# Two attention blocks over eight images: a new order for VectorE's work between attentions, and key-tile sums by transfers in every attention

## The chip, the cores and the metric

The kernel runs on one core of a Trainium2 chip. The metric is the device time of one execution in microseconds (us), the median of several runs. The profile is of one such execution.

## The reference

The input is eight images of 512 channels by 1024 positions, in float32. Two blocks follow each other, with the same computation and different weights:

```python
xn = group_norm(x, 8 groups) * gamma + beta
q, k, v = Wq @ xn + bq, Wk @ xn + bk, Wv @ xn + bv        # 512 x 1024 each
attn = softmax(q^T k / sqrt(64))                          # 8 heads of 64, 1024 x 1024 each
x = x + Wp @ (v attn^T) + bp
```

So there are 16 jobs, an image and a layer each. The kernel goes through them by pairs of images: layer 0 of both, then layer 1 of both.

## The kernel before

**Stages.** A job has a stage of projections and an attention. From job 3 on one stage of projections, called phase n here, makes v of job n, the output projection of job n-1, and k and q of job n, in this order. Every 512x512x1024 product is done with a two-level Strassen-Winograd scheme: seven outer products, each of which is a *chain* of seven inner ones. Phase n has 28 chains: 0 to 6 make v, 7 to 13 the output, 14 to 20 k, 21 to 27 q. Two neighbouring chains are interleaved product by product on TensorE. A product takes some 0.43 us of TensorE.

**A chain** (`chain`, and `deep_phases` with `begin`, `end`, `product` and `put`). Its products come in the order 1, 5, 6, 2, 7, 3, 4 and accumulate in four PSUM banks z, y, u, w. ScalarE copies z to y after product 1, w to an SBUF tile `s5` after product 5 (L780) and z to u after product 6 (L470), and evicts two of the four blocks (L760, L769, L771). In an output, k or q chain VectorE evicts the other two and adds `s5` to them (L776, L778): the block of z after product 7, and the block of u after product 3. Product 4 accumulates in z again, so it waits for VectorE's eviction after product 7; three other products of the interleaved chains stand between the two. In a v chain ScalarE evicts all four, and VectorE adds `s5` once at the end (`add_five`, L801). `s5` comes from a pool of three buffers.

**VectorE's other work in a phase.** The seven chains' results are added to each other in tiles of 128x1024: for v by `plus` (L805, queued in `values`), for the output, k and q by `add` and `more` (L792, L832, queued in `outer`). The output's chains need sums of the attention's result: `plan_sums` lists them in `planned` with a time before which they may not be done, a time by which they are to be done, and the chain before which they must be done (L413 to L419, and L562 to L567 in the tile `os`). Some of the output's parts are added to x by an accumulating transfer on GpSimd's queue instead (L830).

**What sets the order.** The engines' orders are written by hand: the Python code runs along TensorE's products and keeps a `clock` that `advance` moves. `pump` puts VectorE's next work into its queue as long as VectorE is free, by its planned costs, before `clock + AHEAD` (0.8 us). `spend` books those costs: 1.14 us a 128x1024 addition, 0.62 us an `add_five`. VectorE counts as busy for `TAIL` = 9.0 us from the phase's start. `pump` is called at every product of a v chain, and after products 7 and 3 of the other chains. `p_tile` calls for work ahead of its time where no tile is free.

**Attention** (class `Attention`, `run`). It has 64 steps, in 8 groups of 8 key tiles; a group is a pair of heads and half of the queries. In step i TensorE makes the scores of key tile i (L1029) and the values of key tile i-2 (L1080), and ScalarE makes `e`, the exponential (L1034). The softmax's denominators need the sum of the eight `e` of a group. Either VectorE does seven additions (L1048, L1050), or, where `by_transfer` holds, two pairs of the first four `e` are added by an accumulating transfer on GpSimd's queue (`add_pair`, L1057, 512 KB), VectorE adds the other four, and adds the two sums of pairs five steps after each transfer was issued (`LANDING` = 5, L1060). `by_transfer` holds from attention 4 on, but not for the last group of an attention. Then `reduce` (L1115) and the steps after it turn the sum into a factor, which comes back over DRAM on SP's queue to a tile `rb`, and `normalise` multiplies (L1172).

**Buffers.** `e`, the weights of the chains (`w`), the chains' results (`p`) and the weights of `deep_values` share one pool of 12 tiles of 128x1024. `deep_values` prepares the v weights of a layer during attentions 2 and 3: seven times a load, four VectorE additions (L159 to L165) and a store to DRAM. SP's queue issues all loads of weights, the stores of the output and the loads of the next images, in the order of the code.

Of the kernel before, what the change touches and what calls it, by code (L numbers as in the profile page):

```python
# [47 lines left out]
PARTS = 6  # L48
LANDING = 5
BLOCK = {1: (0, 0), 2: (0, 1), 4: (1, 1)}  # L50
AHEAD, TAIL = 0.8, 9.0
PLACE = {2: (0, 0), 6: (0, 1), 5: (1, 1), 7: (1, 0)}
DEEP_V = 3
OUTER_V = (1, 6, 7, 2, 3, 5, 4)
# [24 lines left out]
def fast_path(  # L79
# [522 lines left out]
    def deep_phases(n, extra, outs=None, early=()):  # L602
# [28 lines left out]
        def spend(us):  # L631
            free_at[0] = max(free_at[0], clock[0]) + us

        def next_work(c, forced=False):
            now = clock[0] - began[0] if began else 0.0
            if planned and planned[0][1] <= now and not forced:
                _, _, _, us, fn = planned.popleft()
            elif values:
                us, fn = values.popleft()
            elif planned and planned[0][0] <= now and not forced:  # L640
                _, _, _, us, fn = planned.popleft()
            elif outer:
                fn = outer.popleft()
                us = 0.0 if fn in free else 1.14
            elif extra and extra[0][0] <= c - base:
                us, fn = 0.65, extra.popleft()[1]
            else:
                return False
            fn()
            spend(us)  # L650
            return True

        def pump(c):
            while free_at[0] < clock[0] + AHEAD and next_work(c):
                pass

        def plan_sums():
# [124 lines left out]
        def end(c):  # L782
            which, o = chains[c]
            m = job(which)
            used((m, which, o))

            def p(k):
                return tiles[which, k]

            def add(to_, a, b, frees):  # L790
                def go():
                    nc.vector.tensor_add(to_, a, b)  # L792
                    let_go((which, frees))

                outer.append(go)

            if which == V:
                def add_five():
                    to_ = p(o)[:, 2:4, :].rearrange("p t (o c) -> p t o c", o=2)
                    five = fives[V, o].rearrange("p (t c) -> p t c", t=2).unsqueeze(2)  # L800
                    nc.vector.tensor_add(to_, to_, five.to_broadcast([P, 2, 2, P]))  # L801

                def plus(to_, a):
                    def go():
                        nc.vector.tensor_add(p(to_), p(to_), p(a))  # L805
                        let_go((V, a))

                    values.append((1.14, go))

                values.append((0.62, add_five))  # L810
                for to_, a in {
                    6: ((6, 1),), 7: ((7, 6),), 2: ((2, 1),), 3: ((6, 3),), 5: ((6, 5), (5, 7)),
                    4: ((7, 4),),
                }.get(o, ()):
                    plus(to_, a)
                return

            if which == O:
                b, layer = jobs[m]
                xt = xs[b]  # L820

                def more(oh, sh, part, moved=False):


                    cols = slice(sh * HALF, (sh + 1) * HALF)
                    to_ = xt[:, 2 * oh : 2 * oh + 2, cols]

# [13 lines left out]

                    waiting[oh, sh] += 1
                    if not moved:
                        outer.append(go)
                    elif waiting[oh, sh] == 1:
                        go()
                    else:
                        outer.append(go)
                        free.append(go)

                if o == 1:
                    more(0, 0, 1, m > 0)
                elif o == 2:
                    more(0, 0, 2, True)
                elif o == 6:
                    add(p(6), p(6), p(1), 1)
                    more(0, 1, 6)
                elif o == 5:
                    more(0, 1, 5)
                    more(1, 1, 5, m in (0, 2))  # L860
                elif o == 7:
                    add(p(7), p(7), p(6), 6)
                    more(1, 0, 7)
                    more(1, 1, 7)
# [11 lines left out]
        waiting, free = dict.fromkeys(parts, 0), []  # L876
        soon, outer = deque(early), deque()

        def thunk(c, j):
            def go():  # L880
                if with_v and not began:
                    began.append(clock[0])
                    free_at[0] = clock[0] + TAIL
                if j == 0:
                    live[c] = begin(c)
                order = LAST_ORDER if c + 1 == len(chains) else ORDER
                live[c](order[j])
                if with_v:
                    if chains[c][0] == V:
                        pump(c)  # L890
                    elif order[j] in (7, 3):
# [17 lines left out]
                advance(0.446 if chains[c][0] == V else 0.432)  # L909

            return go

        for which, o in chains[:2]:
            prepare((job(which), which, o))
# [10 lines left out]
        return [thunk(c, j) for c, j in at], plan_sums  # L925

    def last_weights(n):
        w = acts.tile([P, NW, 2, CH], F32, tag="deep", name="w_last")
# [78 lines left out]
    class Attention:  # L1007
        def __init__(self, n):
# [7 lines left out]
            self.spread = n > DEEP_V  # L1016
            self.summed, self.due = {}, {}

        def scores(self, i, tag="sc"):
# [18 lines left out]

        def add(self, i):
            g, kc = self.steps[i]  # L1040
            if self.by_transfer(g):
                if kc < NT // 2:
                    return
                kc -= NT // 2
            acc, e = self.acc, self.es[i]
            if kc == 1:
                acc[g] = apool.tile([P, 2, HALF], F32, tag="acc", name=f"acc_{self.n}_{g}")
                nc.vector.tensor_add(acc[g], self.es[i - 1], e)  # L1048
            elif kc > 1:
                nc.vector.tensor_add(acc[g], acc[g], e)  # L1050

        def by_transfer(self, g):
            return self.spread and g + 1 < len(self.groups)

        def add_pair(self, i):
            g, kc = self.steps[i]
# [1 line left out]

            def add():
                nc.vector.tensor_add(self.acc[g], self.acc[g], self.summed.pop(i))  # L1060
                if kc == NT // 2 - 1:
                    self.reduce(g)

            self.due[i + LEAD + LANDING] = add
# [1 line left out]
        def values(self, i):  # L1066
# [4 lines left out]
            if kc == 0:  # L1071
                po[g] = two_banks("po", f"po_{n}_{g}")
            e = es.pop(i)
            if self.by_transfer(g) and kc < NT // 2:
                self.summed[i] = e
            for h in range(2):
                r = slice(h * HD, (h + 1) * HD)
# [7 lines left out]
        def finish(self, g):  # L1085
# [3 lines left out]


            self.take(g)
            if not self.by_transfer(g):
                self.reduce(g)

        def take(self, g, middle=None):
# [82 lines left out]
        def run(self, chores, between=None, middle=None):  # L1178
# [8 lines left out]
            for i in range(3, len(steps) + LEAD):  # L1187
# [3 lines left out]
                    between()  # L1191
                self.values(i - LEAD)
                g, kc = steps[i - LEAD]
                if self.by_transfer(g) and kc in (1, 3):
                    self.add_pair(i - LEAD)
                if i in self.due:
                    self.due.pop(i)()
# [286 lines left out]
    for n in range(-1, len(jobs)):  # L1484
        last = n + 1 == len(jobs)
        outs = None
        if n >= 0:
# [369 lines left out]
```

## Time and profile before

| | us |
|---|---|
| median of 3 runs (lowest, highest) | 3270.77 (3269.48, 3271.94) |
| the profiled execution | 3270.5 |
| its span, from first to last instruction | 3268.7 |
| VectorE, ScalarE busy | 2728.4, 2077.0 |
| mean granted TensorE clock | 0.992 |

A row of stretches gives for each stretch: its borders, its length, and for each engine the busy time with the number of instructions; then the mean granted clock of TensorE as a share of full speed, the busy share of the 16 DMA engines and what they moved. A row of waits has the waiting engine and line, who ended the wait, the total in us, how often, and the longest. A row of the timeline has start, duration, engine, line, operation, tiles and shapes; in brackets is the engine's idle time before it and who ended that.

Attention n ends where phase n+1 begins; the first products of the phase are mixed into the attention's last steps.

### The profile page before, as it was taken

To read this page: it belongs to the slowest core of one execution; us is meant where nothing else is said; L and a number is where in the kernel's file an instruction comes from. 1 tells how busy PE (TensorE), PEld (TensorE's weight loads), DVE (VectorE), ACT (ScalarE), POOL (GpSimd) and SP (SyncE) were. 2 spreads that over 40 slices of the span, in tenths; PEclk is the share of its full clock that TensorE was granted. 3 is DMA by queue.
4 is the path that set the end of the run, shared out by engine and by line. 5 is a ranking of instruction groups with operands and counts; after the bars stand their busy time and mean duration, and the time that the engine had idled before them with its cause. 6 is when DMAs were issued, how large, how long until landed. Compare 5 with 4: busy or idle time off the path is not lost. (4 is left out here: it accounts for less than half of the span.)

```text
span 3268.7 us, 61316 instructions
## 1 busy us (share of the span) xinstructions
PE 3197.8 (98%) x24009; PEld 1883.6 (58%) x24009; DVE 2728.4 (83%) x4008; ACT 2077.0 (64%) x3583; POOL 233.2 (7%) x262
## 2 busy tenths in 40 slices
PE   9999999899999999999999999999999999999999
PEld 7365483563846638366483654837547375573744
DVE  8897999989879787897978879788797887978867
ACT  4746656565666666666666666666666666666664
POOL 0000000000010010100001000010000100001000
PEclk9999999999999999999999999999999999999999
DMA  7243352443645454455554545445556453444643
GB/s 269 67 130 97 98 174 83 155 146 107 196 89 143 107 137 132 80 154 145 143 173 91 147 98 140 116 92 163 139 134 176 91 174 83 133 118 93 192 106 80
DMA packets 180746, 424.11 MB, mean 130 GB/s; under 512 B 37224, under 2 KB 55264, under 8 KB 180192
## 3 DMA queue, kind: packets, MB, share of 16 engines
q1 hardware_dynamic: 139664, 300.04, 27.7%
q0 software_dynamic: 40784, 120.08, 20.3%
q8 instruction: 190, 3.11, 0.4%
q14 instruction: 108, 0.88, 0.1%
HBM read 246.69 MB, written 52.10 MB: 91 GB/s over the span
## 5 line engine op out<-in xcount | busy, mean ns | idle before, releaser
L1034 ACT ACTIVATE e<-sc 128x1024 f32<-128x1024 f32 x1024 | 1043.7, 1024 | 582.8 <-PE sc L1029 518.6
L1029 PE MATMUL sc<-q,k 64*64 64x512 f32 x8192 | 1062.2, 591 | 15.2 <-ACT e L1034 14.9
L1080 PE MATMUL po<-e,v 64*64 64x512 f32 x8192 | 1062.8, 591 | 0.0
L1029 PEld LDWEIGHTS sc<-q,k 64*64 64x64 f32 x8192 | 311.3, 133 | 582.1 <-issue 515.5
L1080 PEld LDWEIGHTS po<-e,v 64*64 64x64 f32 x8192 | 312.7, 133 | 562.7 <-issue 548.5
L1050 DVE TENSOR_TENSOR acc<-acc,e 128x1024 f32<-128x1024 f32 x432 | 525.5, 1216 | 50.5 <-ACT e L1034 35.0
L1048 DVE TENSOR_TENSOR acc<-e,e 128x1024 f32<-128x1024 f32 x128 | 156.3, 1221 | 123.4 <-ACT e L1034 123.2
L753 PE MATMUL zd<-deep,w 128*128 128x256 f32 x860 | 241.3, 380 | 2.7 <-DVE p L776 1.9
L1057 POOL DMA_DIRECT2D e<-e x168 | 144.5, 860 | 1174.1 <-ACT e L1034 1007.6
L753 PE MATMUL vd<-deep,w 128*128 128x256 f32 x804 | 224.5, 380 | 3.7 <-ACT yd L466 1.5
L1060 DVE TENSOR_TENSOR acc<-acc,e 128x1024 f32<-128x1024 f32 x168 | 204.1, 1215 | 1.3
L753 PEld LDWEIGHTS zd<-deep,w 128*128 128x128 f32 x860 | 162.8, 190 | 27.4 <-DVE p L776 3.1
L830 POOL DMA_DIRECT2D x<-p x61 | 73.4, 1203 | 1386.6 <-ACT p L771 602.5
L753 PEld LDWEIGHTS vd<-deep,w 128*128 128x128 f32 x804 | 152.2, 190 | 26.9 <-ACT yd L466 1.9
L1115 DVE TRANSPOSE_TENSOR_REDUCE r<-acc 128x32 f32<-128x1024 f32 x128 | 159.0, 1243 | 3.3
L753 PE MATMUL zd<-os,w 128*128 128x256 f32 x352 | 100.1, 385 | 33.1 <-DVE p L776 31.5
L780 ACT COPY s<-zd 128x256 f32<-128x256 f32 x209 | 77.9, 373 | 84.9 <-PE zd L753 65.0
L780 ACT COPY s<-vd 128x256 f32<-128x256 f32 x195 | 72.7, 373 | 81.9 <-PE vd L753 58.4
L470 ACT COPY ud<-vd 128x256 f32<-128x256 f32 x209 | 74.6, 357 | 78.4 <-PE vd L753 73.9
L753 PE MATMUL vd<-os,w 128*128 128x256 f32 x368 | 114.9, 397 | 4.0 <-DVE p L778 3.9
L470 ACT COPY ud<-zd 128x256 f32<-128x256 f32 x195 | 70.0, 359 | 70.8 <-PE zd L753 69.6
L748 PE MATMUL vd<-w,deep 128*128 128x128 f32 x780 | 113.1, 278 | 0.0
(308 smaller groups left out, 4725.3 us busy)
## 6 DMA issues: line engine op xcount, KB each, us to landing
w<-deep SPq DMA_DIRECT2D x378, 448.0 KB
e<-e POOLq DMA_DIRECT2D x168, 512.0 KB, 4.6
x<-p POOLq DMA_DIRECT2D x61, 512.0 KB, 5.6
rb<-rd SPq DMA_DIRECT2D x96, 256.0 KB
deep<-w SPq DMA_DIRECT2D x42, 448.0 KB
x<-x_dram SPq DMA_DIRECT2D x28, 512.0 KB
out_dram<-x SPq DMA_DIRECT2D x28, 512.0 KB
w<-keep SPq DMA_DIRECT2D x32, 256.0 KB
```

Of the source, the lines that this page charges most:

```text
L470: nc.scalar.copy(u, z)
L748: nc.tensor.matmul(ps[:, tokens], moving[i][:, tokens], lhs[:, FACTOR[i], :], start=(start and ti == 0), stop=True, skip_group_check=True,)
L753: nc.tensor.matmul(ps, lhs[:, FACTOR[i], :], moving[i], start=start, stop=True, skip_group_check=True,)
L780: return chain(product, lambda ps: nc.scalar.copy(s5, ps), put, z, y, u, w)
L1029: nc.tensor.matmul(sc[h * HD : (h + 1) * HD, j, :], k[r, hp, k0 : k0 + HD], q[r, hp, sh * HALF : (sh + 1) * HALF], start=True, stop=True,)
L1034: nc.scalar.activation(e, sc, AF.Exp, scale=SCALE)
L1048: nc.vector.tensor_add(acc[g], self.es[i - 1], e)
L1050: nc.vector.tensor_add(acc[g], acc[g], e)
L1057: nc.gpsimd.dma_start(self.summed[i], self.summed.pop(i - 1), accum_op=ALU.add)
L1060: nc.vector.tensor_add(self.acc[g], self.acc[g], self.summed.pop(i))
L1080: nc.tensor.matmul(po[g][j * HD : (j + 1) * HD, h, :], v[r, kc, d0 : d0 + HD], e[r, j, :], start=(kc == 0), stop=(kc == NT - 1),)
L1115: nc.vector.tensor_reduce(self.r[:, 0, m, :], self.acc.pop(g).rearrange("p j (b e) -> p (j b) e", e=RP), AX.X, ALU.add, apply_transpose=True,)
```

## The change

In the phases from job 3 on:

- VectorE counts as busy for 12.0 us from the start, a 128x1024 addition is booked with 1.22 us, an `add_five` with 0.72 us.
- `pump` is called at every product of every chain, with a limit: the time up to which VectorE has to be free for its next eviction after a product 7, plus `SLACK` = 1.3 us. Work of `values`, `outer` and `extra` that doesn't fit before the limit is not placed; the planned sums are not held back by it.
- The `add_five` of chains 0 and 1 are placed at once.

In the attentions: two pairs of every group but the last are summed by transfers in every attention, also in 0 to 3. In the last attention four additions for the last projection are placed three steps later each.

```diff
-AHEAD, TAIL = 0.8, 9.0
+AHEAD, TAIL, SLACK = 0.8, 12.0, 1.3
-        def next_work(c, forced=False):
+        def next_work(c, forced=False, limit=None):
             now = clock[0] - began[0] if began else 0.0
+            room = 9.9 if limit is None else limit - max(free_at[0], clock[0])
...
             elif values:
+                if values[0][0] > room:
+                    return False
                 us, fn = values.popleft()
...
             elif outer:
+                if room < 1.22 and outer[0] not in free:
+                    return False
                 fn = outer.popleft()
-                us = 0.0 if fn in free else 1.14
-            elif extra and extra[0][0] <= c - base:
+                us = 0.0 if fn in free else 1.22
+            elif extra and extra[0][0] <= c - base and room > 0.65:
...
-        def pump(c):
-            while free_at[0] < clock[0] + AHEAD and next_work(c):
+        def pump(c, limit):
+            while free_at[0] < clock[0] + AHEAD and next_work(c, limit=limit):
...
-                    values.append((1.14, go))
-
-                values.append((0.62, add_five))
+                    values.append((1.22, go))
+
+                if c < 2:
+                    add_five()
+                    spend(0.72)
+                else:
+                    values.append((0.72, add_five))
...
-                    if chains[c][0] == V:
-                        pump(c)
-                    elif order[j] in (7, 3):
+                    if chains[c][0] != V and order[j] in (7, 3):
                         spend(0.38)
-                        pump(c)
+                    pump(c, limits[i] and clock[0] + limits[i])
...
+        limits, limit = [], None
+        for c, j in reversed(at):
+            limits.append(limit)
+            if chains[c][0] != V and (LAST_ORDER if c + 1 == len(chains) else ORDER)[j] == 7:
+                limit = takes(c) + SLACK
+            if limit is not None:
+                limit += takes(c)
+        limits.reverse()
...
-        def by_transfer(self, g):
-            return self.spread and g + 1 < len(self.groups)
+        def pairs(self, g):
+            return 0 if g + 1 == len(self.groups) else 2
...
-                    put(46 + 3 * i, fn)
+                    put(49 + 3 * i, fn)
```

More of the change, by code (lines that the diff above doesn't have):

```diff
@@ L806, in go @@
                         let_go((V, a))
-                    values.append((1.14, go))
-                values.append((0.62, add_five))
-                for to_, a in {
+                    values.append((1.22, go))
[4 more added lines that the diff above has]
+                    values.append((0.72, add_five))
+                for step in {
                     6: ((6, 1),), 7: ((7, 6),), 2: ((2, 1),), 3: ((6, 3),), 5: ((6, 5), (5, 7)),
@@ L814, in end @@
                 }.get(o, ()):
-                    plus(to_, a)
+                    plus(*step)
                 return
@@ L877, in deep_phases, with thunk @@
         soon, outer = deque(early), deque()
-        def thunk(c, j):
+        def thunk(i, c, j):
             def go():
@@ L908, in go, with takes @@
                         assert not values and not planned
-                advance(0.446 if chains[c][0] == V else 0.432)
+                advance(takes(c))
             return go
+        def takes(c):
+            return 0.446 if chains[c][0] == V else 0.432
         for which, o in chains[:2]:
@@ L924, in deep_phases @@
             ]
-        return [thunk(c, j) for c, j in at], plan_sums
+        limits, limit = [], None
[6 more added lines that the diff above has]
+        limits.reverse()
+        return [thunk(i, c, j) for i, (c, j) in enumerate(at)], plan_sums
     def last_weights(n):
@@ L1015, in __init__ @@
             self.es, self.acc, self.po = {}, {}, {}
-            self.spread = n > DEEP_V
             self.summed, self.due = {}, {}
@@ L1040, in add @@
             g, kc = self.steps[i]
[L1041 to L1044, printed above, removed]
+            first = 2 * self.pairs(g)
+            if kc < first:
+                return
+            kc -= first
             acc, e = self.acc, self.es[i]
@@ L1060, in add @@
                 nc.vector.tensor_add(self.acc[g], self.acc[g], self.summed.pop(i))
-                if kc == NT // 2 - 1:
+                if kc == 2 * self.pairs(g) - 1:
                     self.reduce(g)
@@ L1073, in values @@
             e = es.pop(i)
-            if self.by_transfer(g) and kc < NT // 2:
+            if kc < 2 * self.pairs(g):
                 self.summed[i] = e
@@ L1091, in finish @@
             self.take(g)
-            if not self.by_transfer(g):
+            if not self.pairs(g):
                 self.reduce(g)
@@ L1193, in run @@
                 g, kc = steps[i - LEAD]
-                if self.by_transfer(g) and kc in (1, 3):
+                if kc % 2 == 1 and kc < 2 * self.pairs(g):
                     self.add_pair(i - LEAD)
```

## The prediction

> **What bounds the kernel now.** I read the page's shares first, then the waits, then stretches stage by stage, then the timeline where a wait stood. TensorE is busy almost all of the span:
>
> ```profile
> PE 3197.8 (98%) x24009; PEld 1883.6 (58%) x24009; DVE 2728.4 (83%) x4008; ACT 2077.0 (64%) x3583; POOL 233.2 (7%) x262
> ```
>
> Its products are the same, in the same order, in both kernels, and so is ScalarE's work. So the change can win only what TensorE loses now: some 71 us idle, and time at a lower clock. The waits name two places:
>
> ```profile
> PE zd L753 <- DVE p L776: 34.0, 16, 3.8
> PE sc L1029 <- ACT e L1034: 14.9, 6, 4.7
> ACT e L1034 <- DVE acc L1050: 18.7, 14, 5.1
> ACT e L1034 <- DMA deep<-w_values: 6.8, 3, 5.1
> ```
>
> The first is a product 4 of a chain that waits for VectorE's eviction; the others are scores that wait for ScalarE, and ScalarE for a tile that VectorE or a store still holds. The stretches tell which stages pay. They are attentions 2, 3 and 4, then phases 4, 6 and 3:
>
> ```profile
> 489.80:608.80 119.00, 111.41 (x1018) 38.80 (x1017) 112.75 (x153) 73.01 (x76) 1.43 (x1) 0.99 0.34 111
> 701.10:822.70 121.60, 114.25 (x1018) 39.42 (x1017) 115.66 (x157) 73.06 (x76) 1.42 (x1) 0.96 0.28 86
> 910.70:1019.90 109.20, 109.20 (x1018) 38.79 (x1017) 93.22 (x114) 73.32 (x76) 12.60 (x15) 1.00 0.50 109
> 824.80:910.70 85.90, 85.51 (x490) 76.69 (x486) 67.43 (x116) 58.69 (x154) 4.80 (x4) 1.00 0.60 176
> 1223.30:1313.40 90.10, 87.37 (x490) 78.01 (x490) 69.96 (x119) 58.22 (x154) 4.80 (x4) 0.98 0.45 128
> 610.90:701.20 90.30, 85.80 (x490) 76.58 (x488) 73.66 (x146) 58.70 (x154) 6.00 (x5) 1.00 0.64 198
> ```
>
> The same work takes 109.2 us in attention 4, where TensorE never stops, and 9.8 and 12.4 us more in attentions 2 and 3, where VectorE is busy 95% (112.75 of 119.00). Attentions 0 and 1 take 110.1 us with TensorE busy throughout. Phase 4 takes 85.9 us, phase 6 4.2 us more. The eleven phases 5 to 15, by the same stretches, last 991.7 us together, against 11 x 85.9 = 944.9: 46.8 us more. In the timeline of phase 6 this has one place:
>
> ```profile
> 1247.67 0.68 DVE L801 TENSOR_TENSOR v<-v,s 128x512 f32<-128x512 f32 x1
> 1248.45 2.48 DVE L805 TENSOR_TENSOR v<-v 128x1024 f32<-128x1024 f32 x2
> 1250.86 0.42 DVE L776 TENSOR_TENSOR p<-zd,s 128x256 f32<-128x256 f32 x1
> ```
>
> ```profile
> 1251.33 0.70 PE L753 MATMUL zd<-os,w 128*128 128x256 f32 x2 [2.48 <-DVE p L776]
> ```
>
> VectorE, without a pause since the attention's tail, does three items of v before the first output chain's eviction (1250.86), and product 4 waits 2.48 us.
>
> **The price of such a stall** is more than its length: the four us after it are at a lower clock.
>
> ```profile
> 1251.30:1255.40 4.10, 4.07 (x13) 3.36 (x14) 2.68 (x5) 1.57 (x4) 1.20 (x1) 0.67 0.09 16
> ```
>
> Clock 0.67 for 4.1 us loses 1.35 us by the clock; against phase 4, product by product, it is 1.67 us. The Trainium skill ("TensorE: Matmul & The Clock Gate", Part 1 on the clock gate) has the clock drop only after an idle window of about 3.4 us. By that a 2.48 us stall costs only itself, and eleven phases could win 11 x 2.5 = 27 us. The stretches give 46.8; I take them.
>
> **The order of VectorE, phases 5 to 15.** Nothing is added or removed; I walked the new order with the distances from start to start that this timeline shows (128x1024: 1.14 us, 1.2 where two follow on one tile; `add_five` 0.60, or 0.79 if its sum follows; `os` 0.34 to 0.45; evictions 0.34 and 0.40), beside the product times of stall-free phase 4. Up to the first `add_five` (1232.67) the order is the old one. The three items above (3.19 us) move behind the eviction, so VectorE is free for it at 1250.86 - 3.19 = 1247.67. Product 7 ends at about 1247.5 and product 4 is wanted at 1248.85: the eviction ends at 1248.1, and the stall goes.
>
> What is late next: the `add_five` of chain 3 moves from 1240.87 to 1242.1, that of chain 4 from 1244.27 to 1245.3. They hold `s5`, so ScalarE's copies of `s5` of chains 6 and 7, now at 1241.87 and 1245.04, come at 1242.9 and 1246.0. Behind each stand an eviction and the copy of z to u (0.37 us each) that product 7 waits for: ready at 1244.0 and 1247.15, wanted at 1243.8 and 1246.85. That is 0.25 and 0.35 us. The `add_five` of chain 5 now stands behind chain 8's evictions, so chains 7, 8 and 9 share one `s5` buffer, and ScalarE's copy waits for the chain before; there 0.2 to 0.35 us are left. Chain 11's eviction has two sums of v before it, 0.13 us late; the later ones with two 128x1024 before them (chains 14, 15, 19, 26) end with 0.05 us to spare. Sum: 0.7 us a phase. Bounds: 0, if the stalls absorb each other, and 2.
>
> Queues that this passes: the additions to x come some 7 us earlier beside the products, so the accumulating transfers and the output's stores too. With them the four loads of the next image, in the phases that have them, now stand in SP's queue ahead of four loads of q weights. In phase 4 the last transfer would land at about 881 instead of 887.7; a store takes 4.6 us (887.7 to 892.3), so the loads go out at 885.5. In phase 7 these 2 MB and two weights (448 KB each) were in 10.4 us after the first issue (1496.1 to 1506.5, where the DMA share falls); 2 MB and one weight scale to 9 us, so they land at 894.5; chain 24 wants them at 897.2. So it costs 0, and up to 2 us in each of six phases if transfer and store are both slow.
>
> Phases 5 to 15: 46.8 - 11 x 0.7 = 39.1 us won. Phase 4 has no stall now, since attention 3 before it left VectorE free earlier; with that attention changed its tail is like the others': 0.7 lost. Phase 3 has seven preparations of weights (L159 to L165, 1 us each) that the plan doesn't book: the walk gives stalls of 2.6, 1.2, 0.7, 0.6 and 0.7 us, 5.8 together, where it now has 3.8. 2.0 lost.
>
> **Attentions 0 to 3.** In seven groups of each, seven additions become five: 14 x 1.216 = 17.0 us less VectorE work. In attentions 0 and 1 that is worth nothing, TensorE hides it. In 2 and 3 VectorE comes to 95.8 and 98.7 us of 109.2, beside 93.2 in attention 4, which has no stall. From the timelines, the running sum there begins up to 12 us behind the `e` it adds (group 6), in attention 4 at most 4. The four preparations of v weights in the last groups (0.96 us each) are what attention 4 lacks, so I expect a lag of 5 to 6 us. A weak point stays: the exponential of step 57 takes the tile of a prepared weight whose store is issued only at step 54 or so; with a lag of 3 us and a store of 3 us ScalarE waits 1 to 2 us. I take 1 us of TensorE in each: (9.8 - 1) + (12.4 - 1) = 20.2 won; bounds 8 and 22.
>
> 56 more transfers go through GpSimd's queue (0.86 us each, engine idle); what could be late is their landing, for VectorE waits for it in order, five steps (8.55 us) after the issue:
>
> ```profile
> e<-e POOLq DMA_DIRECT2D x168, 512.0 KB, 4.6
> DMA to landing us min/median/max: 4.5/4.6/7.2
> ```
>
> The Trainium skill ("DMA: Bandwidth & Descriptors", SWDGE vs HWDGE vs iDMA) speaks against it: an engine alternates between queues of GpSimd and of SP, and attentions 0 to 2 begin with 1 to 2 MB of weights. Twice 4.6 is 9.2, 0.65 too late. But those loads are over 10 us into the attention (DMA share 0.73 up to 93 us, 0.01 after it), and the first sum is wanted 14 us in. Free VectorE time covers the rest.
>
> SP's small loads of factors fall behind one store or weight load each in attentions 0 to 3, and the last attention's four additions come three steps later: VectorE's freed time and TensorE's last products cover both; 0.5 us without that.
>
> **Sum.** The profiled execution took 3270.5 us, 1.8 around its span, 0.3 under the median. 39.1 - 0.7 - 2.0 + 20.2 = 56.6 less is 3213.9, in terms of the median 3214.
>
> **Rivals.** *The stall only moves* (0.08). If VectorE runs 1 us later than walked, the late `s5` copies stop TensorE at chains 6 to 9 by 1 us each: phases win nothing, 3270.5 - 20.2 + 2.7 = 3253. For it: margins of 0.2 us. Against: the walk gives 2.5 us for the present stall, and VectorE works 70 of 90 us.
> *Attentions 2 and 3 stay bound* (0.12): by tiles, not by VectorE. For it: the 5.1 us wait for a store. Against: that store was late because VectorE was. 8 instead of 20.2: 3226.
> *Slower* (0.04): the transfers of attentions 0 to 3 land late. VectorE there averages 108.1 - 17.0 = 91.1 us busy; to lose the phases' 36.4 us each must last 115.2 + 9.1 = 124.3, so 33 us of waits in 14 sums, 2.4 each: it decides from 8.55 + 2.4 = 10.9 us to landing. At 12 us: 91.1 + 48.3 = 139.4, four times 24 longer, 3330. Against: 7.2 at most so far.
>
> **The numbers.** The main case has 0.76, alone 3203 to 3226. From 3203 (nothing left of either loss) to 3232 (attentions bound, some loads late) holds about 0.82. A measurement of this kernel tells 0.2% (6.5 us) from no change: faster in the main case and two rivals, less what lies between, 0.94; same 0.02; slower 0.04.
>
> **What would show it.** Right: phases 5 to 15 at 86 to 87 us, clock 1.00, the wait of zd for p nearly gone except in phase 3; attentions 2 and 3 at 109 to 111 us; 224 transfers at 4.6 us. Wrong: waits of ScalarE's `s` for p or v over 1 us, of TensorE for weights in phases 4, 7, 8, 11, 12, or of VectorE for e.

## The result, and the profile after

The changed kernel takes 3255.18 us (median, 3252.26 to 3257.79), the kernel before, on the same chip, 3270.05 us (3269.15 to 3271.94). The ratio is 0.9954, with a 95% interval of 0.9939 to 0.9968: faster by some 15 us, where 56.6 were forecast, and outside the range of 3203 to 3232. The profiled execution took 3257.8 us (before: 3270.5), its span is 3256.0.

The shares of the page say little: TensorE's busy time hardly moved (3197.8 before), and VectorE has 56 instructions fewer, the additions that became transfers.

```profile
PE 3195.4 (98%) x24009; PEld 1863.8 (57%) x24009; DVE 2673.1 (82%) x3952; ACT 2055.6 (63%) x3583; POOL 279.7 (9%) x318
```

The stretches of the changed kernel, in the same columns as before: attentions 2, 3 and 4, then phases 4, 6, 3 and 7.

```profile
489.70:609.30 119.60, 112.62 (x1018) 39.01 (x1017) 97.49 (x138) 72.65 (x76) 12.78 (x15) 0.97 0.66 171
703.90:817.60 113.70, 111.17 (x1018) 38.96 (x1017) 95.95 (x138) 73.16 (x76) 12.61 (x15) 0.98 0.62 153
907.70:1016.90 109.20, 109.20 (x1018) 38.79 (x1017) 89.27 (x110) 73.26 (x76) 12.59 (x15) 1.00 0.51 107
819.70:907.80 88.10, 86.41 (x490) 76.36 (x490) 73.80 (x123) 56.99 (x154) 4.77 (x4) 1.00 0.59 176
1218.80:1307.40 88.60, 86.91 (x490) 76.30 (x490) 74.38 (x123) 56.66 (x155) 4.77 (x4) 1.00 0.46 130
611.30:704.00 92.70, 87.91 (x490) 75.87 (x488) 77.42 (x148) 57.15 (x154) 5.99 (x5) 1.00 0.63 193
1418.60:1509.20 90.60, 87.24 (x490) 76.14 (x488) 74.63 (x123) 56.64 (x154) 4.77 (x4) 1.00 0.58 173
```

Phase 6 went from 90.1 to 88.6, not to 86.7; attention 2 didn't move although VectorE's busy time there fell from 112.75 to 97.49; attention 3 lost 7.9 of its 12.4 us over attention 4. Stage by stage, from the two profiled executions:

| | before | after | forecast | measured |
|---|---|---|---|---|
| phases 5 to 15 together | 991.6 | 978.9 | -39.1 | -12.7 |
| phase 4 | 86.0 | 88.1 | +0.7 | +2.1 |
| phase 3 | 90.3 | 92.7 | +2.0 | +2.3 |
| attention 2 | 119.0 | 119.6 | -8.8 | +0.6 |
| attention 3 | 121.6 | 113.7 | -11.4 | -7.9 |
| attentions 4 to 14 | 1202.3 | 1203.0 | 0 | +0.7 |
| behind attention 15 | 32.4 | 34.6 | 0 | +2.2 |

With 0.1 less in the rest this is the 12.7 us by which the two spans differ. Of the last row 0.6 us is a longer wait of the last projection for VectorE, the rest lies behind the last product and varies by that much between executions of kernels that share it (the row is 32.0 to 34.6 us in the experiments below).

The waits of the whole kernel (zd and vd are banks that TensorE's products write, p, q and k are tiles that the evictions fill, s is `s5`):

```profile
PE zd L758 <- DVE p L783: 21.3, 29, 0.8
DVE q L797 <- ACT q L774: 21.9, 26, 0.8
ACT s L785 <- DVE p L806: 30.4, 25, 2.0
PE vd L758 <- DMA w<-deep: 2.3, 3, 1.5
PE sc L1046 <- ACT e L1051: 10.1, 4, 5.4
ACT e L1051 <- DMA deep<-w_values: 16.9, 4, 7.5
DVE q L1189 <- DMA rb<-rd: 24.2, 17, 6.5
```

The 16 waits of up to 3.8 us of zd for p are gone, and with them the slow clock that followed ten of the eleven stalls in phases 5 to 15. In their place are 29 of at most 0.8 us, two of 0.79 in each of the 13 phases. The place of the first one in phase 6, at the change from k's chain 18 to chain 19:

```profile
1278.52 0.42 DVE L781 TENSOR_TENSOR k<-ud,s 128x256 f32<-128x256 f32 x1 [0.44 <-PE ud L758]
1279.78 2.48 DVE L797 TENSOR_TENSOR k<-k 128x1024 f32<-128x1024 f32 x2 [0.84 <-ACT k L774]
1282.19 0.48 DVE L783 SCALAR_TENSOR_TENSOR p<-zd,bias_step,s 128x256 f32<-128x256 f32 x1
```

```profile
1282.72 0.70 PE L758 MATMUL zd<-deep,w 128*128 128x256 f32 x2 [0.79 <-DVE p L783]
```

VectorE is done with chain 18's last eviction at 1278.94. The two sums that the plan placed next read a block of k that ScalarE copies only at 1279.38 to 1279.75, so VectorE stands still for 0.84 us; the eviction that product 4 waits for begins at 1282.19 instead of 1281.35.

### The profile page after: what moved, and what is told of

Its sections match the earlier page's. It is cut to its first block, busy times and chain, and to the rows that moved or that the text cites. A ratio compares the mean times of both kernels' runs of the same rounds, so it can differ in the third digit from the quotient of the medians.

```text
span 3256.0 us, 61327 instructions
## 1 busy us (share of the span) xinstructions
PE 3195.4 (98%) x24009; PEld 1863.8 (57%) x24009; DVE 2673.1 (82%) x3952; ACT 2055.6 (63%) x3583; POOL 279.7 (9%) x318
## 4 chain that ended last, share of the span: by engine, by line
PE 82%; DVE 10%; DMA 4%; issue 2%; ACT 1%; SPq 0%; POOL 0%; DVEq 0%; ACTq 0%; POOLq 0%
PE sc L1046 25%; PE po L1097 24%; PE zd L758 8%; PE vd L758 8%; PE yd L758 3%; PE vd L753 3%; PE ud L758 3%; PE zd L753 3%; DVE acc L1067 1%; PE ud L753 1%; PE yd L753 1%; DMA x<-p 1%; PE z L522 1%; DVE k L797 1%; DMA w<-deep 1%
## 5 line engine op out<-in xcount | busy, mean ns | idle before, releaser
L1067 DVE TENSOR_TENSOR acc<-acc,e 128x1024 f32<-128x1024 f32 x320 | 389.4, 1217 | 49.9 <-ACT e L1051 41.7
L1074 POOL DMA_DIRECT2D e<-e x224 | 192.2, 858 | 1750.2 <-ACT e L1051 1394.8
L1077 DVE TENSOR_TENSOR acc<-acc,e 128x1024 f32<-128x1024 f32 x224 | 272.1, 1215 | 1.9
L1120 DVE TENSOR_TENSOR q<-po,px 128x512 f32<-128x512 f32 x115 | 78.3, 681 | 48.9 <-ACT px L1118 48.8
```

The source lines that it names most:

```text
L1074: nc.gpsimd.dma_start(self.summed[i], self.summed.pop(i - 1), accum_op=ALU.add)
```

## Experiments: the phases

**One half of the change at a time.** The order without the new transfers:

```diff
-            return 0 if g + 1 == len(self.groups) else 2
+            return 0 if g + 1 == len(self.groups) or self.n <= DEEP_V else 2
```

> The changed kernel with the transfers of attentions 0 to 3 taken back (seven additions on VectorE a group, as before); the new order stays. Theory: the order alone wins some 1.5 us in each of phases 5 to 15 (88.6 us, each with two stalls of 0.8 us of zd for p), loses 2 us in phase 3 and 2 us in phase 4 (88.1), and attentions 2 and 3 stay at 119.0 and 121.6: 3270 - 17 + 4 + some loads of weights that come late (4) = about 3261. Rival, the order's part of the prediction (phases at 86.7): 3234. Second rival: the transfers are what makes the order work, and without them the 2.5 us stall behind the attention is back: 3270 or more.

Measured: 3261.6 us, ratio 0.9972 (0.9964 to 0.9981). Phase 6 is 88.58, as with the transfers, attentions 2 and 3 are 120.0 and 121.6. The transfers without the order, on the kernel before:

```diff
-            self.spread = n > DEEP_V
+            self.spread = True
```

> The kernel before with the two pairs by transfer in attentions 0 to 3 too; the order of VectorE in the phases stays the old one. Theory: attention 3 falls from 121.6 to about 114, attention 2 stays at 119 to 120 since VectorE waits there for the broadcast of the reciprocals, phase 4 gets the 2.5 us stall of the others (90.1 instead of 86.0): 3270 - 7.5 + 4 = about 3267. Rival, the attentions' part of the prediction without the phase: attentions 2 and 3 at 110, 3270 - 20 + 4 = 3254.

Measured: 3265.8 us, ratio 0.9988 (0.9981 to 0.9994). Attention 3 falls to 112.8, attention 2 stays at 118.6, phase 6 at 90.10; phase 4 gets the 2.48 us stall of the others and rises from 86.0 to 89.0, and phase 3 rises from 90.3 to 93.9. The two halves win 8.7 and 4.4 us, 13.1 together, and the whole 15; each falls short in its own place. Whether they act on each other these times don't tell, since attention 2 alone varies by 3 us between executions (below).

**The stalls at chains 19 and 26.** The plan books ScalarE's delay, and nothing else changes:

```diff
+            if with_v:
+                spend(0.84)
             for to_, a in {
                 2: ((2, 1),), 6: ((6, 1),), 7: ((7, 6), (6, 5), (5, 7)), 3: ((6, 3),), 4: ((7, 4),),
```

> The changed kernel; the plan also books 0.84 us at the end of each chain of k and q, the time by which the first of its sums waits for ScalarE's eviction, so that no longer two 128x1024 sums are placed ahead of the eviction of the next product 7. Theory: the two stalls of 0.79 us at chains 19 and 26 go, each worth 0.95, in 13 phases: 13 x 1.9 = 24.7 less than the changed kernel, 3230; phase 6 at 86.7. Rival: the stalls come from late copies of s5 or from the clock, or the displaced sum makes product 3 of the same chain late by as much: phase 6 stays at 88.6 and the time within 4 us of the changed kernel's 3255.

Measured: 3235.2 us, ratio 0.9895 (0.9879 to 0.9910). The timeline of phase 6 shows one sum ahead of the eviction now, the other behind it:

```profile
1277.65 1.23 DVE L797 TENSOR_TENSOR k<-k 128x1024 f32<-128x1024 f32 x1 [0.24 <-ACT k L774]
1278.80 0.48 DVE L783 SCALAR_TENSOR_TENSOR p<-zd,bias_step,s 128x256 f32<-128x256 f32 x1
1279.41 0.48 DVE L783 SCALAR_TENSOR_TENSOR p<-ud,bias_step,s 128x256 f32<-128x256 f32 x1
1279.81 1.21 DVE L797 TENSOR_TENSOR k<-k 128x1024 f32<-128x1024 f32 x1
```

Product 4 no longer waits there. Phases 5 to 15 fall from 978.9 to 957.0 together, 2.0 each, and phase 6 alone by 2.2, where 1.9 was expected. The whole misses 3230: products of phases 3, 4, 7, 8, 11 and 12 now come before their weights, with 8.4 us of waits against 2.3 in the changed kernel. Of this kernel's waits:

```profile
PE vd L758 <- DMA w<-deep: 8.4, 6, 2.0
PE zd L758 <- DVE p L783: 0.8, 3, 0.3
```

The plan's own constant does it as well:

```diff
-AHEAD, TAIL, SLACK = 0.8, 12.0, 1.3
+AHEAD, TAIL, SLACK = 0.8, 12.0, 0.7
```

> The changed kernel with the plan's SLACK at 0.7 instead of 1.3, nothing else: the room ahead of the next product 7 falls from 3.0 to 2.4 us, so one 128x1024 sum is placed there instead of two, the other between the evictions of products 7 and 3. Theory: the 0.79 us stalls at chains 19 and 26 go as with the booked wait (3235), if the sum between the two evictions costs less than 0.5 us a chain: 3232 to 3240. Rival: that sum takes 1.14 us where 0.86 lie between the evictions, and ScalarE's copy to u and product 7 of the next chain wait instead: 3245 or more.

Measured: 3232.7 us, ratio 0.9878 (0.9863 to 0.9893), phase 6 at 86.21. The 0.84 us wait is still there, but only one sum follows it. When the sums of chain 18 are queued, three products are left up to the end of the next product 7. With 1.3 the plan sees 1.3 + 3 x 0.432 = 2.60 us of room, and two sums at 1.22 fit into it; with 0.7 it sees 2.00, and only one fits (the 3.0 and 2.4 of the expectation count one product too many). So the number of sums ahead of that eviction decides.

**The copies of s5.** Each fourth chain's `s5` takes a tile of the same size that only attentions use:

```diff
-            s5 = small.tile([P, QT], F32, tag="s5", name=f"s5_{n}_{c}", bufs=3)
+            if with_v and c % 4 == 3:
+                s5 = small.tile([P, NQ, 2, RP], F32, tag="r", name=f"s5_{n}_{c}", bufs=1)
+                s5 = s5.rearrange("p a b c -> p (a b c)")
+            else:
+                s5 = small.tile([P, QT], F32, tag="s5", name=f"s5_{n}_{c}", bufs=3)
```

> The changed kernel with a fourth buffer for s5 in the phases with v (each fourth chain uses the attention's idle tile r of the same size). Theory: the 0.7 to 1.1 us that chains 5 to 9 lose against the stall-free phase come from copies of s5 that wait for an add_five of three chains before; with four buffers they go, in 12 phases: 8 to 13 us less than the changed kernel, 3242 to 3247, and the two stalls at chains 19 and 26 stay at 0.79 us. Rival: these shifts have another cause, phase 6 stays at 88.6 and the time at 3255.

Measured: 3243.1 us, ratio 0.9922 (0.9908 to 0.9935). Phase 6 falls from 88.58 to 87.75; ScalarE's wait for an `add_five` (now L810), 30.4 us before, is

```profile
ACT s L789 <- DVE p L810: 1.1, 1, 1.1
PE zd L762 <- DVE p L787: 21.4, 29, 0.8
```

and the 29 stalls are untouched. So the late copies cost 0.83 us a phase, where the forecast had 0.7.

**The loads of the next image.** On the kernel with the wait booked:

```diff
-                    ahead.append((11, lambda b=jobs[n][0] + 2: (x_tile(b), load_x(b))))
+                    ahead.append((16, lambda b=jobs[n][0] + 2: (x_tile(b), load_x(b))))
```

> The kernel with the 0.84 us booked (3235), and the loads of the next image at chain 16 instead of chain 11 of the phases that have them. Theory: the waits of products for weights there (1.87 in phase 4, 1.77 in 7, 0.63 in 8, 0.68 in 11, 1.45 in 12) come from the four loads of x that stand ahead of four loads of q weights in SP's queue and wait for a store; behind those weights they cost nothing: phases 4, 7 and 12 at 88.3, 3235 - 8 = 3227. Rival: the weights are late by the accumulating transfers and stores themselves, or x comes late for the next attention's statistics: 3235 or more.

Measured: 3222.4 us, ratio 0.9854 (0.9839 to 0.9869). No product waits for `w<-deep` any more in these phases, phase 7 is 86.3 (88.4 without this edit, 90.6 in the changed kernel). Of the 11.5 us between the profiled executions with and without this edit, 9.9 lie in phases 3 to 15. Attention 2, which ends before the first of these loads, differs by 2.9 us, which is scatter. SP's queue now issues the loads of x and of q weights in turn, where all four of x stood first.

## Experiments: attentions 2 and 3

In both, TensorE stops before the score of step 59, because ScalarE can't begin the exponential of step 57: its tile held the last prepared v weight, whose store has not landed. The preparations earlier by three steps, or by four with their loads, on the changed kernel:

```diff
-                        put(29 + 4 * i, lambda o=o: make(o))
+                        put(26 + 4 * i, lambda o=o: make(o))
```

> The changed kernel; in attentions 2 and 3 the preparations of v weights stand three steps (5.1 us) earlier in VectorE's order (their loads stay where they are). Theory: step 57's exponential waits for the store of the last prepared weight (7.5 us in attention 2, 4.6 in attention 3), so both waits go when that store is issued 5 us earlier: attention 3 from 113.7 to about 109.5, attention 2 from 119.6 to 112 to 115; 3255 - 10 = 3245. Rival: VectorE now waits for the loads of those weights in order, or the tile is late for another reason: attentions 2 and 3 within 1 us of the changed kernel's, 3255.

```diff
-                        put(23 + 4 * i, lambda o=o: load(o))
-                        put(29 + 4 * i, lambda o=o: make(o))
+                        put(19 + 4 * i, lambda o=o: load(o))
+                        put(25 + 4 * i, lambda o=o: make(o))
```

> The changed kernel; loads and preparations of v weights in attentions 2 and 3 both four steps (6.8 us) earlier, so that VectorE has no more to wait for loads than now. Theory: step 57's exponential waits because the last preparation, planned at step 53, comes as late as VectorE's lag (some 6 us in attention 3, 10 in attention 2), and its store takes 2.3 to 2.5 us more; four steps earlier it is in time in attention 3 (113.7 to 109.5 or 110.5) and nearly in attention 2 (119.6 to 113 to 116): 3255 - 8 = 3247. Rival, as with the preparations alone: waits in VectorE's order take its place, attention 3 stays at 113 or more, 3253 or more.

Both are slower than the changed kernel: 3264.3 us, ratio 0.9982 (0.9974 to 0.9990), and 3265.9 us, ratio 0.9985 (0.9978 to 0.9992). Attentions 2 and 3 take 125.4 and 116.3 us, and 121.4 and 120.7. In the first VectorE waits in its order for the loads, as the rival had it (attention 2, below), and in the second it still does in attention 3, 2.9 and 2.8 us:

```profile
559.42 0.29 DVE L159 TENSOR_TENSOR w_values<-w_values 128x128 f32<-128x128 f32 x1 [2.90 <-DMA w_values<-keep]
578.01 0.29 DVE L159 TENSOR_TENSOR w_values<-w_values 128x128 f32<-128x128 f32 x1 [3.84 <-DMA w_values<-keep]
```

The wait for the reciprocals, taken away in attention 2 alone:

```diff
-            times = (0.0, 0.2, 2.0, 4.0) if ends else (0.0, 7.6, 7.7, 16.2)
+            times = (0.0, 0.2, 2.0, 4.0) if ends else (0.0, 7.6, 7.7, 22.2 if n == DEEP_V - 1 else 16.2)
```

> The changed kernel; in attention 2 alone the multiplication by the broadcast reciprocals is placed 22.2 instead of 16.2 planned us behind the reduction. Theory: VectorE's 6.5 us wait for rb at 537 us is where attention 2's freed VectorE time went (rb lands late behind the 1.8 MB store of factors issued at 528); without it VectorE's lag falls by about 6 us, the last weight is made that much earlier, and attention 2 falls from 119.6 to 113.7 to 115.5, as attention 3, while attention 3 stays at 113.7: 3255 - 5 = 3250. Rival: VectorE catches up by itself, and attention 2 is bound by the place of the preparations in its order: no change, 119.6 and 3255.

Measured: 3253.9 us, ratio 0.9949 (0.9935 to 0.9962), which the interval doesn't tell from the changed kernel. Attention 2 took 116.3 us; executions of kernels that share the changed kernel's attention 2 have it at 116.9 to 119.8, so the gain may be scatter. VectorE's 6.5 us wait at 537 has become two others:

```profile
539.32 1.23 DVE L1065 TENSOR_TENSOR acc<-e,e 128x1024 f32<-128x1024 f32 x1 [2.90 <-ACT e L1051]
543.38 0.29 DVE L159 TENSOR_TENSOR w_values<-w_values 128x128 f32<-128x128 f32 x1 [2.84 <-DMA w_values<-wqkv_dram]
```

Next, three sums of the normalised image (L451 to L457) moved from ahead of the last preparation to behind it, which itself isn't moved:

```diff
-                    for at, fn in zip((41, 43, 45, 47, 49, 51, 53, 55), deep_first):
+                    late = (54, 56, 58, 60) if n <= DEEP_V else (49, 51, 53, 55)
+                    for at, fn in zip((41, 43, 45, 47) + late, deep_first):
```

> The changed kernel; in attentions 2 and 3 the last four sums of the normalised image (128x768, 0.87 us from start to start) stand at steps 54 to 60 instead of 49 to 55, so three of them, 2.6 us, no longer stand ahead of the last preparation of a v weight; nothing of the preparations or their loads is moved. Theory (VectorE's queue makes the store late): that preparation comes 2.6 us earlier, at 799 instead of 801.6 in attention 3, its store lands near 802.2 instead of 804.9, the wait of step 57 falls from 4.6 to 2 us of ScalarE and from 2.5 to near 0 of TensorE: attention 3 from 113.7 to 109.5 to 110.5, attention 2 from 119.6 to 115 to 117; 3255 - 6 = 3249. Rival (the ring of tiles alone): the waits stay, attention 3 at 113 or more, 3255.

Measured: 3258.1 us, ratio 0.9961 (0.9948 to 0.9975). The preparation does come at 798.9 in attention 3, but attention 3 still takes 111.7 us, and phases 3 and 4 lose 2.2 and 3.7 us to the late sums. The store was issued only at 801.1, behind three gathers in SP's queue. So in addition the last store went to GpSimd's queue:

```diff
-            later(1.0, lambda: nc.sync.dma_start(keep, w))
+            queue = nc.gpsimd if o == OUTER_V[-1] else nc.sync
+            later(1.0, lambda: queue.dma_start(keep, w))
```

> As the kernel with the four sums of the normalised image later, and the store of the last prepared v weight issued by GpSimd instead of SP. Theory (SP's queue): there the preparation came 2.6 us earlier (798.9 in attention 3) but its store was issued only at 801.1, behind three gathers of the reduction in SP's queue; GpSimd, idle by then, issues it at 800 and it lands at 802.5 to 803: attention 3 from 111.7 to 109.3 to 110.3, attention 2 from 117.6 to 114 to 115.5. Phases 3 and 4 keep what the later sums cost them (96.9 and 93.8), 3258 - 4 = 3254. Rival (the store itself takes 5 us or more beside the accumulating transfers and loads of that moment): attention 3 at 111.5 or more.

Measured: 3259.1 us, ratio 0.9962 (0.9948 to 0.9976). The intervals of these two runs don't tell them from the changed kernel. In attention 3, which took 114.4 us, the store lands at 804.0, and ScalarE waits 4.9 us all the same, from the exponential of step 57, which runs in time, to that of step 58. VectorE's and ScalarE's timelines of that kernel (lines one higher than in the changed kernel):

```profile
804.25 0.59 DVE L1160 TENSOR_REDUCE lt<-r 32x64 f32<-32x256 f32 x1 [2.76 <-DMA r<-r]
...
807.15 1.23 DVE L1078 TENSOR_TENSOR acc<-acc,e 128x1024 f32<-128x1024 f32 x1
```

```profile
808.46 1.94 ACT L1052 ACTIVATE e<-sc 128x1024 f32<-128x1024 f32 x2 [4.87 <-issue]
```

The page names no releaser. The program does: step 58's tile held the sum of the pair of steps 48 and 49 that a transfer made, and comes free when VectorE has added it. That addition ends at 808.38 and the exponential begins at 808.46. In the changed kernel the two tiles come free one behind the other:

```profile
805.18 1.02 ACT L1051 ACTIVATE e<-sc 128x1024 f32<-128x1024 f32 x1 [4.59 <-DMA deep<-w_values]
807.47 1.94 ACT L1051 ACTIVATE e<-sc 128x1024 f32<-128x1024 f32 x2 [0.79 <-PE sc L1046]
```

```profile
806.18 1.21 DVE L1077 TENSOR_TENSOR acc<-acc,e 128x1024 f32<-128x1024 f32 x1
```

The same instant in the other kernels, the end of that addition and the start of step 58's exponential (us):

| | attention 2 | attention 3 |
|---|---|---|
| changed kernel | 597.80, 597.88 | 807.39, 807.47 |
| preparations earlier | 602.62, 602.70 | 813.41, 813.49 |
| with their loads | 598.42, 598.50 | 814.09, 814.17 |
| sums later | 595.64, 595.72 | 807.05, 807.13 |

Always 0.08 us apart. In the lower three rows, and with GpSimd's store, step 57 doesn't even take the prepared weight's tile: each edit shifts the order in which the code hands the tiles out, so those runs could not test that store. What they show is the second tile. Whatever becomes of the store, step 58 waits for VectorE's addition, and that comes late because VectorE still is. In attention 3 of the changed kernel it works from 783 to 808 us with 0.2 us of pauses in all; in attention 2, and in the edits, it also stands in its order before loads, gathers and reciprocals, and has no free time behind to make up for it.

## Experiments: the edits together

The wait booked, the loads, the fourth `s5` and the preparations three steps earlier:

> All of it together on the changed kernel: the 0.84 us booked, the fourth s5, the preparations three steps earlier, the loads of x at chain 16. Theory: the gains add, since each takes away a wait at another place: 3255 - 20 - 12 - 8 - 10 = 3205, with phases 5 to 15 near 87.4 between attentions (stretch of products 85.5 to 86). Rival: chains 5 to 9, once faster, make VectorE late at chains 11 to 26 again, and half of the s5 gain is lost: 3211.

Measured: 3223.2 us, ratio 0.9855 (0.9839 to 0.9870): phases 5 to 15 at 941.6 us together, 85.6 each, and attentions 2 and 3 at 125.2 and 118.2. Without the earlier preparations:

> The changed kernel with the 0.84 us booked, the fourth s5 and the loads of x at chain 16 (the preparations where the changed kernel has them). Theory: the phases as with all four changes (963 us for phases 5 to 15 between attentions, against 973 without the fourth s5), the attentions as in the kernel with two of them (117 and 112): 3222 - 10 = 3211. Rival: attention 2 loses what the phases win: 3218 or more.

Measured: 3214.1 us, ratio 0.9823 (0.9810 to 0.9837). Its phase 6:

```profile
1209.10:1294.70 85.60, 85.55 (x490) 76.89 (x490) 73.01 (x122) 58.39 (x155) 4.77 (x4) 1.00 0.48 136
```

TensorE is without a pause; that is less than phase 4 of the kernel before, which the forecast took as free of stalls. Three combinations with the edits for the attentions shown above followed: on top of the three, the shift of loads and preparations with the later multiplication in attention 2; the later sums; the later sums with the later multiplication.

> The three, with loads and preparations of v weights four steps earlier and the reciprocals' multiplication 6 us later in attention 2. Theory: phases as with the three (3211), attention 3 at 110, attention 2 at 111 to 114: 3211 - 6 = 3205. Rival: VectorE's waits in order only change their place in attention 2, which stays at 116 or more: 3209 to 3212.

> The kernel with the three changes (0.84 us booked, fourth s5, loads at chain 16; 3214) and the four sums of the normalised image later in attentions 2 and 3. Theory: attention 3 at 110, attention 2 at 114 to 116, the phases unchanged: 3214 - 6 = 3208. Rival: the sums are late for the first products of phases 3 and 4, which lose what the attentions win: 3212 to 3216.

> The same, and the multiplication by the reciprocals 6 us later in attention 2. Theory: with VectorE's queue shorter ahead of the last preparation, the 6.5 us wait for the reciprocals counts in attention 2: 112 to 114 there, 3208 - 2 = 3206. Rival: VectorE waits for the first prepared weight's load instead, as when this was done alone: no change against the kernel without it.

Measured: 3219.6 (0.9842, 0.9828 to 0.9855), 3214.3 (0.9827, 0.9814 to 0.9841) and 3211.8 us (0.9821, 0.9808 to 0.9835). The first loses attention 3 (120.7) as the shift alone did. The second wins 2 us in attention 2 and loses 3 in phase 3. In the third attentions 2 and 3 are 114.4 and 111.8, but phases 3 and 4 take 94.4 and 89.6. The last is the fastest kernel here, 58.9 us under the kernel before, but its interval doesn't set it apart from the one with three edits.

## Why the prediction was wrong

Of the forecast 56.6 us the profiled executions show 12.7. Of the 43.9 that are missing, 26.4 lie in phases 5 to 15, 12.9 in attentions 2 and 3, 1.7 in phases 3 and 4, and the rest elsewhere. Two steps failed: the margin of 0.05 us at chains 19 and 26, and the 1 us for each of attentions 2 and 3.

**Phases 5 to 15: the mechanism was right, the residue was not.** The stall of 2.48 us went in all eleven phases, and the slow clock behind it in the ten that had it. What failed is the sentence that chains 14, 15, 19 and 26 "end with 0.05 us to spare". For 19 and 26 this margin is right only if the two 128x1024 sums begin right behind VectorE's last eviction, when VectorE is free. Their operand wasn't there: it comes from ScalarE, 0.84 us later. A margin of 0.05 against a wait of 0.84 gives a stall of 0.79 us. Product by product, against phase 6 of the kernel with three edits, it costs 0.95 us at the product that waits and 0.11 at the next. Twice in eleven phases this is 23 us of the 26.4 that are missing. Booking the wait removed it and brought 2.0 us a phase. The plan in the code makes the same error: it knows when VectorE is free, not when an operand is there.

The late copies of `s5` at chains 6 to 9 were found, and nearly sized: 0.83 instead of 0.7 a phase, 1.4 us in all. The loads of x ahead of the q weights were costed at 0, with up to 2 us in each of six phases: phase 7 lost 2.1, a wait of 1.46 for its weights among them, phase 3 waited 0.6 and phase 11 0.2, phase 12 lost 0.2, and phases 4 and 8 nothing. The cover was thin: with phases 2 us shorter TensorE waits for weights in all six, 0.6 to 2.0 us each. Phases 10 to 12 lost another 2.4 us against the other phases: 0.58 each at one product of v's chains, where ScalarE's copy of `s5` had waited 1.73 us for an `add_five` (phases 11 and 12 had this loss before, too), and 0.7 at the weights of phases 11 and 12. The terms of this account are then 23.2 for the stalls, 1.4, 2.1, 2.4, and 1.2 for 0.11 a phase at chain 16. Against them stand 4.7 us, for phase 4, the forecast's measure, itself loses 0.43 us in the output's chains that the new order doesn't. That makes 25.6; the stretches, rounded to 0.1 us each, give 26.4.

**Phases 3 and 4.** Phase 3's loss has the size forecast (2.3 for 2.0), but by chance, for its parts are others: instead of stalls of 2.6, 1.2, 0.7, 0.6 and 0.7 us it has the two of 0.79 at chains 19 and 26, 0.63 for weights, and 0.8, 0.4, 0.4 and 0.5. Phase 4 did become like the others, but by the residue of the others, 2.1 instead of 0.7, the same two stalls.

**Attentions 2 and 3: the step "I take 1 us of TensorE in each" failed.** It contradicts its own numbers. It expected a lag of VectorE of 5 to 6 us, and priced the store's tile at a lag of 3. In attention 3 the running sums begin up to 5.3 us behind their `e` in group 6, as expected, ScalarE waits 4.6 us, and TensorE loses 2.5 and then four us at clock 0.64. The rival that these two attentions stay bound by tiles had the size: 8 us for both, where 7.3 are measured. Of its reason one half holds, the tiles; "not by VectorE" doesn't, since both tiles come free behind late work of VectorE. Its time was not right for the whole, since the phases fell short too. And the store was not the only late tile: behind it stands the addition of a transferred pair, which no view of the kernel before could show in these attentions, since it is new there, but which the text could have placed, with the tile that it frees. Attention 2 won next to nothing although VectorE got 15 us less to do: the two executions with the old attention took 119.0 and 120.0 us, the six with the new one 116.9 to 119.8. The trace shows VectorE standing 6.5 us before the reciprocals, which it used to reach late enough (1.8 at most in the kernel before):

```profile
DVE q L1172 <- DMA rb<-rd: 10.8, 11, 1.8
```

Without that wait it stood before an exponential and a load. How the 10 us of attention 2 divide among these was not separated.

**The other steps.** The 56 new transfers cost nothing as such: 224 land in 4.6 us by the median and 8.2 at most, within the 8.55 at hand, and attentions 0 and 1 are unchanged. The last attention's later additions cost 0.6 us at the last projection, for which the text had 0, or 0.5 without cover. The rival that the stall only moves named 3253, close to the measured time, but by chains 6 to 9 losing 1 us each; they lose 0.8 us together, and the stall moved elsewhere. The rival *slower* did not come true. Of the signs named for being wrong two came: ScalarE's waits for an `add_five` of over 1 us (2.0 at most), and TensorE's wait for weights in phase 7 (1.5).

## What to carry to other kernels

When a planned order is walked by hand, or by a planner, let each instruction start at the later of two times: when its engine is free and when its operands are there. When an engine gets less to do, list what it will wait for in its order at the earlier time, and which buffers come free only behind it: of two buffers due at the same moment the trace names one, and the other is there when the first is mended.

## What the runs showed of the hardware

A pause of TensorE of 0.79 us cost 0.95 us, and 0.11 at the next product, with the clock at 1.00 in the 4.1 us behind it. One of 2.53 us in attention 3 was followed by 4.1 us at clock 0.64, as the 2.48 us one in phase 6 of the kernel before was by 4.1 us at 0.67. But the same stall of 2.48 us in phase 12 of the kernel before, which ends at 2461.63, was followed by clock 1.00 (the last row), and one of 3.78 us in its phase 3 as well:

```profile
1282.70:1286.80 4.10, 4.08 (x19) 3.62 (x20) 3.50 (x5) 2.31 (x6) 0.00 (x0) 1.00 0.04 11
806.30:810.40 4.10, 4.10 (x28) 1.16 (x32) 4.10 (x5) 2.32 (x3) 0.00 (x0) 0.64 0.81 229
2461.60:2465.70 4.10, 4.07 (x19) 3.60 (x20) 3.45 (x8) 2.24 (x6) 1.20 (x1) 1.00 0.11 21
```

Product by product the stall in phase 12 cost 1.7 us less than the one in phase 6, which is what the prediction gave the slow clock (1.67).

The traces of all 18 kernels here, from 20 us on, have 80 pauses of 0.95 to 1.82 us, and none was followed by a lower clock in the next 4.1 us. All 16 pauses of 3.89 us and more were, with 0.50 to 0.63. Of the 65 between, 45 were, the shortest of 1.86 us; what decides there these runs don't show. So in this kernel a long stall mostly costs more than short ones of the same sum. The rule of the Trainium skill ("TensorE: Matmul & The Clock Gate", Part 1), that the clock drops after an idle window of about 3.4 us, which the prediction weighed and left, doesn't describe the pauses of 1.86 to 2.53 us that a lower clock followed.
